# 113 matmuls of constants put between the work of a two-layer recurrent block

## The chip, the cores and the metric

The kernel runs on one core of one Trainium2 chip. The metric is the time of one execution in device microseconds (us). The engines are named as in the profile: PE is TensorE (PEld its weight loads), DVE VectorE, ACT ScalarE, POOL GpSimd, SP the queue that issues most DMAs.

## The reference

The input x has shape (2, 2048, 256) in fp32. There are two layers; each normalises x, sends it through two branches, and adds the product of the first with the silu of the second. Cut to what matters:

```python
xn = layernorm(x)
s = local_and_latent_attention(xn)          # 16 heads, window 128
g = silu(mixture_of_experts(xn))            # 8 experts, each token goes to one
x = x + s * g
xn = layernorm(x)
s = block_attention_and_mlp(xn)             # 16 heads, blocks of 64, MLP of 1024
g = silu(two_layer_local_transformer(xn))   # 8 heads of 64, window 128, depth 2
x = x + s * g
```

All arithmetic is fp32.

## The kernel before

The 4096 tokens are 32 tiles of 128 rows (NT), taken in 8 groups of four tiles (NG, GT). The program has three stages, one after another:

1. The first layer (lines 379 to 960). For every group `head` projects queries, keys and latents, `attention` scores and sums, tile by tile and half tile by half tile; `prep` normalises, transposes and routes the tokens; `route` works out each token's place; `send` scatters the normalised rows, one tile per indirect DMA on POOL (L547), into expert order; `expert` runs 39 expert tiles beside the attention of the later groups.
2. The dense branch of the second layer (968 to 1366), two transformer layers with 16 rounds of four tiles in all (NR, NM = 64 tiles): `gate_head` forms the input of a round, `prepare` projects and rotates a tile, `attention` and `forward` follow.
3. The attention branch of the second layer (1379 to 1647): again `head`, `attention`, `forward` in 8 rounds, and the store of the output.

The passage from stage 1 to 2 and from 2 to 3 is what the change's short name calls a change of branch.

The order of instructions on every engine is the order in which the program records them; no scheduler moves them. It is made by `in_turn` (L90): it takes lanes, each with a start a, an end b and a list of steps with weights, gives each step the place a + (b - a) x (weight so far + half its own) / (sum of weights), sorts all steps of all lanes by that place, and runs them. The unit is a round, so a lane (0, 1, ...) spreads over the first one. Every engine works its own list strictly in that order, and waits for others by semaphores.

```python
order.append((a + (b - a) * (at + w / 2) / total, i, len(order), do))
...
for _, _, _, do in sorted(order, key=lambda x: x[:3]):
    do()
```

PSUM is dealt out by `bank` (L43): tiles named acc have 2 buffers, all others (s for matmul results, tp for transposes) share 6 in rotation, so that the seventh tile waits until the first was read. A constant array cst (128 x 448: the identity and two masks) is the first load of the program (L48).

```python
def bank(tag):
    return ps.tile([P, 512], F32, name=tag, tag="acc" if tag == "acc" else "b", bufs=2 if tag == "acc" else 6)
```

Lines that the prediction names. Stage 1: L445 transposes of normalised rows; L453 router logits; L489 counts for the route; L204 and L214 projections of queries and keys; L682, L698, L711 and L735 latents; L228 values; L114 scores; L107 mask and row minimum on DVE (tiles pr, mn, mnl); L136 exponentials on ACT; L151 transposes of the weights; L71 and L69 copies out of PSUM on DVE and ACT (tile pt); L165 weighted sums; L188, L252 and L261 the way to the output; L580 the experts' input. Stage 2: L368 transposes of a round's input; L1087 and L1103 projections; L1066 transposes; L1120 and L1131 rotation and row norm on POOL; L341 the gather of expert rows; L1189 division; L1280 transposes, L1297 and L1319 the two halves of the MLP (tile h2T its input). Stage 3: rg is the load of a group, L1425 its transposes, L1601 and L1614 the MLP.

Of the kernel before, what the change touches and what calls it, by code (L numbers as in the profile page):

```python
# [14 lines left out]
NT = B * S // P  # L15
# [3 lines left out]
NG = NT // GT  # L19
# [11 lines left out]
def kernel(ctx: ExitStack, tc: tile.TileContext, io: dict, col: dict):  # L31
    nc = tc.nc
# [14 lines left out]
    cst = sb(const, [P, io["cst"].shape[1]], "cst")  # L47
# [15 lines left out]
    ysort = rmem.tile([FT * P, D], F32, name="ysort")  # L63
    ati = const.tile([P, NT], I32, name="ati", tag="ati")


    def copy(i, out, in_):
        if i % 2:
# [21 lines left out]
    def in_turn(*lanes):  # L90

        order = []
        for i, (a, b, lane) in enumerate(lanes):
            total, at = sum(w for w, _ in lane), 0.0
            for w, do in lane:
                order.append((a + (b - a) * (at + w / 2) / total, i, len(order), do))
                at += w
        for _, _, _, do in sorted(order, key=lambda x: x[:3]):
            do()
# [279 lines left out]
    with ExitStack() as l0_ctx, tc.manual_schedule(engines=ordered):  # L379
# [49 lines left out]
        def prep(g):  # L429

            d = {}
            xg = xn[:, g * GT : (g + 1) * GT, :]
            xT = xT_of(g)
            o = oh[:, g * GT : (g + 1) * GT, :]

            def moments(t):
                if not t:
                    d["mv"] = sb(xp, [P, GT, 2], "ln_mv", 3)
                    d["rs"] = sb(xp, [P, GT], "ln_rs", 3)
                ln_moments(xp, d["mv"], t, [xg[:, t, :]])  # L440

            def turn(c):
                tp = bank("tp")
                for t in range(GT):
                    nc.tensor.transpose(tp[:, t * P : (t + 1) * P], xg[:, t, c * P : (c + 1) * P], ident)  # L445
                copy(c, xT[:, c, :], tp)

            def logits():

                lg = d["lg"] = bank("s")[:, 0 : GT * E].rearrange("p (t e) -> p t e", t=GT)  # L450
                for t in range(GT):
                    for k in range(2):
                        nc.tensor.matmul(  # L453
                            lg[:, t, :],
                            lhsT=xT[:, k, t * P : (t + 1) * P],
                            rhs=wr[:, k, :],
                            start=(k == 0),
                            stop=(k == 1),
                        )
                mx = sb(xp, [P, GT], "mx", 2)  # L460
                nc.vector.tensor_reduce(mx, lg, AX.X, ALU.max)
                nc.vector.tensor_tensor(o, lg, bc(mx, 2, [P, GT, E]), ALU.is_equal)
                nc.vector.tensor_tensor(o, o, bc(desc, 1, [P, GT, E]), ALU.mult)
                nc.vector.tensor_reduce(mx, o, AX.X, ALU.max)
                nc.vector.tensor_tensor(o, o, bc(mx, 2, [P, GT, E]), ALU.is_equal)

            lane = [(1, lambda t=t: moments(t)) for t in range(GT)]
            lane += [(1, lambda: ln_rsqrt(d["rs"], d["mv"], 1e-5)), (2, lambda: None)]
            lane += [(1, lambda t=t: normalize(xg[:, t, :], xg[:, t, :], d["mv"], d["rs"], t)) for t in range(GT)]
            lane += [(1, lambda c=c: turn(c)) for c in range(2)] + [(1, lambda: None), (1, logits)]  # L470
            return lane
# [380 lines left out]
        def finish(n):  # L852

            d = outs[n]

            def take():
                acc = accs.pop(n)
                d["aT"] = sums_out(pa, acc)
                zs = zss[n]
                nc.vector.tensor_scalar(zs, zs, 1e-30, None, ALU.max)  # L860
                nc.vector.reciprocal(zs, zs)

            def divide():
                d["o"] = divided(pa, d["aT"], zss.pop(n))

            lo = lambda: d["o"].rearrange("p b v s d -> p (b v s) d")

            def weigh():
                d["g1"] = sb(pa, [P, 16, 16], "g1")
                nc.gpsimd.tensor_tensor(d["g1"], lo(), bc(gl, 1, [P, 16, 16]), ALU.mult)  # L870
                nc.gpsimd.tensor_tensor(d["g1"], d["g1"], d["g2"], ALU.add)
                nc.gpsimd.tensor_tensor(lo(), lo(), d["rem"], ALU.subtract)

            def gate():
                d["gate"] = sb(pa, [P, 16], "gate")
                nc.vector.tensor_reduce(d["gate"], d["g1"], AX.X, ALU.add)
                nc.scalar.activation(d["gate"], d["gate"], AF.Exp, scale=-1.0)

            def mix():
                nc.vector.tensor_scalar(d["gate"], d["gate"], 1.0, None, ALU.add)  # L880
                nc.vector.reciprocal(d["gate"], d["gate"])
                nc.vector.tensor_tensor(lo(), lo(), bc(d["gate"], 2, [P, 16, 16]), ALU.mult)
                nc.gpsimd.tensor_tensor(lo(), lo(), d["rem"], ALU.add)

            def back():
                d["oT"] = turned_out(pa, d["o"].rearrange("p b v s d -> p b (v s d)"))

            def out():
                s = sb(pa, [P, D], "s")
                nc.vector.tensor_tensor(s, times_out(d["oT"], outw), bout, ALU.add)  # L890
                nc.sync.dma_start(rows_s[:, n, :], s)
                del outs[n]

            return [take, divide, weigh, gate, mix, back, out]
# [27 lines left out]
                lane += [(0.4, back), (0.7, none), (0.3, ahead[1]), (0.7, none), (0.5, out), (0.5, none)]  # L922
            return lane

        in_turn((0, 1, prep(0)), (0.5, 1.5, prep(1)), (0.9, 1.8, head(0)))
        project_values(0)
        score(0)
        score(1)
# [6 lines left out]
        for g in range(NG):  # L935
            lanes = [(0, 1, attention(g))]
            if g < NG - 1:
                lanes.append((0.05, 0.75, head(g + 1)))
            if g == 0:
                lanes += [(0.3 * k, 0.3 * k + 0.35, prep(2 + k)) for k in range(3)]  # L940
            if g == 1:
                lanes += [(0.16 * k, 0.16 * k + 0.25, prep(5 + k)) for k in range(3)]
                lanes += [(0.6, 0.68, route()), (0.7, 1, sends[0:11])]
            if g == 2:
                lanes.append((0, 0.56, sends[11:]))
                lanes.append((0.57, 0.62, [(1, open_experts)] + [(1, lambda: expert_load(0))]))
            share, due = [], weight * shares[g]
            while flow and (due > 0 or g == NG - 1):
                due -= flow[0][0]
                share.append(flow.pop(0))  # L950
            if share:
                lanes.append((1 - shares[g] if g == 2 else 0, shares[g] if g == NG - 1 else 1, share))
            if g == NG - 2:
                lanes.append((0.5, 1, [(1, lambda: load_wqkv(0))]))
            if g == NG - 1:
                (_, fetch), *rest = gate_head(0)
                lanes += [(0.3, 0.4, [(1, fetch)]), (0.77, 1, rest)]
            in_turn(*lanes)
        for step in ends[NT - 1]:
            step()  # L960
# [7 lines left out]
    with tc.tile_pool(name="pd", bufs=2, side="left") as pd, tc.manual_schedule(engines=ordered):  # L968
# [374 lines left out]
            return lane  # L1343

        load_rest()
        in_turn((0, 1, prepare(0)), (0.8, 1.8, prepare(1)))
        score(0)
        lanes = []
        for r in range(NR):
            lanes.append((r, r + 1, attention(r)))  # L1350
            ahead = [prepare(m) for m in range(GT * r + 2, min(GT * r + GT + 2, NM))]
            if r == NG - 1:

                ahead.insert(2, [(0, lambda: load_wqkv(1)), (8, lambda: None)])
            if r == NR - 1:
                ahead.append([(1, lambda j=j: turn_tile(NM - 1, j)) for j in range(2)])
            lanes.append((r, r + (1 if r < NR - 1 else 0.5), sum(ahead, [])))
            if r < NR - 1:
                lanes.append((r, r + 0.45, gate_head(r + 1)))
            if r < NR - 3:  # L1360
                lanes.append((r + 1.25, r + 2.65, forward(r)))
        lanes += [(NR - 1.75, NR - 0.56, forward(NR - 3)), (NR - 0.75, NR - 0.24, forward(NR - 2))]
        lanes.append((NR - 0.24, NR, forward(NR - 1, 0, 2)))
        in_turn(*lanes)
        in_turn((0, 0.5, finish(NM - 1)), (0, 1, forward(NR - 1, 2, 1)))
        in_turn((0, 1, forward(NR - 1, 3, 1)))
    cw_qkv = sb(wq, [P, 2, 3 * D], "d_wqkv")
    nc.sync.dma_start(cw_qkv, io["L1_attn_w_qkv"].rearrange("(k p) n -> p k n", p=P))
    cw_out = sb(wd, [P, 2, D], "d_wo")
# [9 lines left out]
    with tc.tile_pool(name="pc", bufs=2, side="left") as pc, tc.manual_schedule(engines=ordered):  # L1379
# [249 lines left out]
            lane += [(0, lambda t=t: again(t)) for t in ts]  # L1629
            return lane + [(3.4, lambda t=t: narrow(t)) for t in ts]  # L1630

        in_turn((0, 1, head(0)))
        project_values(0)
        score(0)
        score(1)
        lanes = []
        for g in range(NG):
            lanes.append((g, g + 1, attention(g)))
            if g < NG - 1:
                lanes.append((g + 0.02, g + 0.72, head(g + 1)))  # L1640
            if g < NG - 3:
                lanes.append((g + 1.27, g + 2.6, forward(g)))
        lanes += [(NG - 1.73, NG - 0.6, forward(NG - 3)), (NG - 0.73, NG - 0.25, forward(NG - 2))]
        lanes.append((NG - 0.24, NG, forward(NG - 1, 0, 2)))
        in_turn(*lanes)
        in_turn((0, 0.6, [(1, step) for step in ends[NT - 1]]), (0, 1, forward(NG - 1, 2, 1)))
        in_turn((0, 1, forward(NG - 1, 3, 1)))


def _constants():  # L1650
# [141 lines left out]
```

## Time and profile before

| | |
|---|---|
| time, median of 3 runs | 3057.86 us (3057.32 to 3060.87) |
| time of the profiled execution | 3057.81 us |
| its span, first to last instruction | 3056.0 us |
| mean granted clock of TensorE | 0.947 |
| busy: PE, PEld | 2743.0 us (90%), 1979.2 us (65%) |
| busy: DVE, ACT, POOL | 1884.3 (62%), 1675.5 (55%), 1064.8 us (35%) |
| matmul records | 28250, of 15996 matmuls |

An fp32 matmul leaves two records, a transpose one. The page gives each engine's busy time, then the span in 40 equal slices of 76 us, each digit a tenth; the row PEclk is the clock that TensorE was granted. Where a view gives a row as `line engine op x count`, the count is of records. Waits are put down to what ended them.

### The profile page before, as it was taken

How to read it: one execution, taken by the hardware profiler on the slowest of the kernel's cores; microseconds unless marked ns; L12 is line 12 of the kernel's file. 1: busy time of each engine (PE TensorE's matmuls, PEld its weight loads, DVE VectorE, ACT ScalarE, POOL GpSimd, SP SyncE). 2: the span in 40 equal slices, each digit the busy share in tenths (PEclk: the TensorE clock that was granted, in tenths of full speed). 3: DMA queues.
4: the chain of work that ended last, by engine and by line, in shares of the span. 5: the costliest groups of instructions: out<-in, count | busy, mean ns of one | idle time of the engine just before them, and what ended most of it. 6: DMA issues, size and time to landing. Idle time of an engine off the chain costs nothing.

```text
span 3056.0 us, 72578 instructions
## 1 busy us (share of the span) xinstructions
PE 2743.0 (90%) x28250; PEld 1979.2 (65%) x28250; DVE 1884.3 (62%) x6708; ACT 1675.5 (55%) x4598; POOL 1064.8 (35%) x1227
## 2 busy tenths in 40 slices
PE   7875999999985789999999999999998689999997
PEld 4553888888872556656666666666666556666666
DVE  6774555556553777776676676666665366665542
ACT  4554666768772444444444444555553367776772
POOL 1224233323333554554443443444342112222212
PEclk8887999999996899999999999999999889999999
DMA  5002322222212010110000010000000100010000
GB/s 173 14 28 70 132 96 93 100 95 96 100 60 83 26 29 22 29 29 27 14 19 29 15 38 8 8 8 5 2 5 15 53 15 13 25 32 22 19 15 21
DMA packets 88417, 128.63 MB, mean 42 GB/s; under 512 B 8173, under 2 KB 78220, under 8 KB 83084
## 3 DMA queue, kind: packets, MB, share of 16 engines
q1 hardware_dynamic: 85004, 115.60, 11.8%
q0 software_dynamic: 3072, 8.39, 0.9%
q8 instruction: 225, 3.69, 0.5%
q14 instruction: 116, 0.95, 0.1%
HBM read 88.58 MB, written 27.00 MB: 38 GB/s over the span
## 4 chain that ended last, share of the span: by engine, by line
PE 30%; DVE 6%; issue 6%; POOL 4%; ACT 4%; DMA 0%; SPq 0%; POOLq 0%; DVEq 0%; ACTq 0%
PE s L1297 7%; PE s L1319 3%; PE s L1087 3%; ACT pr L1490 3%; PE s L1614 2%; PE s L1601 2%; PE s L1215 2%; POOL inv L1131 1%; PE s L1103 1%; PE acc L1042 1%; POOL scr L1120 1%; PE s L1012 1%; PE tp L151 1%; PE s L214 1%; PE tp L1066 1%
## 5 line engine op out<-in xcount | busy, mean ns | idle before, releaser
L1032 ACT ACTIVATE pr<-pr,mn 128x192 f32<-128x192 f32 (+2 forms) x512 | 188.6, 439 | 276.2 <-DVE mn L107 275.9
L1131 POOL TENSOR_TENSOR inv<-inv,nhalf 128x16 f32<-128x16 f32 x64 | 188.4, 2944 | 414.3 <-DVE inv L1130 414.3
L107 DVE CUSTOM_DVE_ANT_0 pr<-s,cst 128x128 f32<-128x128 f32 (+2 forms) x1024 | 261.6, 316 | 92.2 <-PE s L1470 71.4
L1297 PE MATMUL s<-h2T,d_w 128*128 128x512 f32 (+2 forms) x792 | 314.8, 552 | 0.6 <-DVE h2T L1287 0.6
L69 ACT COPY pt<-tp 128x384 f32<-128x384 f32 (+3 forms) x320 | 156.4, 495 | 247.3 <-PE tp L151 227.4
L151 PE MATMUL tp<-cst,pr 128*128 128x128 f32 x1488 | 220.0, 285 | 60.9 <-ACT pr L1032 51.2
L136 ACT ACTIVATE pr<-pr,mn 128x192 f32<-128x192 f32 (+2 forms) x512 | 222.8, 436 | 71.2 <-DVE mn L107 70.8
L1490 ACT ACTIVATE pr<-pr,mn 128x128 f32<-128x128 f32 x512 | 198.1, 388 | 111.0 <-DVE mn L107 110.7
L1120 POOL TENSOR_TENSOR scr<-scr,tab 128x512 f32<-128x512 f32 x128 | 176.9, 1382 | 201.7 <-DVE scr L71 201.6
L151 PEld LDWEIGHTS tp<-cst,pr 128*128 128x128 f32 x1488 | 180.2, 147 | 101.6 <-ACT pr L1032 56.9
L1087 PE MATMUL s<-d_wqkv,hT 128*128 128x512 f32 x512 | 245.4, 623 | 0.0
L71 DVE COPY pt<-tp 128x384 f32<-128x384 f32 (+3 forms) x320 | 181.6, 567 | 101.6 <-PE tp L151 72.9
L1297 PEld LDWEIGHTS s<-h2T,d_w 128*128 128x128 f32 x792 | 143.5, 194 | 141.5 <-issue 135.4
L1310 DVE SCALAR_TENSOR_TENSOR u<-s,cols,ge 128x512 f32<-128x512 f32 (+2 forms) x108 | 73.9, 689 | 199.4 <-PE s L1297 124.2
L1319 PE MATMUL s<-d_w,u 128*128 128x256 f32 x768 | 178.0, 382 | 0.0
L165 PE MATMUL acc<-pt,v 64*32 64x128 f32 x4992 | 125.3, 294 | 44.6 <-DVE pt L71 28.5
L1087 PEld LDWEIGHTS s<-d_wqkv,hT 128*128 128x128 f32 x512 | 98.8, 204 | 99.5 <-issue 98.7
L611 PE MATMUL s<-Wo,it 128*128 128x128 f32 x1248 | 159.5, 283 | 0.8 <-ACT it L603 0.8
L1319 PEld LDWEIGHTS s<-d_w,u 128*128 128x128 f32 x768 | 142.8, 190 | 22.3 <-issue 3.1
L611 PEld LDWEIGHTS s<-Wo,it 128*128 128x128 f32 x1248 | 150.1, 196 | 9.1 <-issue 7.1
L1619 POOL TENSOR_TENSOR y<-y,stream 128x256 f32<-128x256 f32 x32 | 23.4, 730 | 370.4 <-DVE y L1618 370.4
L107 DVE CUSTOM_DVE_ANT_0 pr<-s,cst_a 128x192 f32<-128x192 f32 (+2 forms) x512 | 144.0, 347 | 8.9 <-PE s L114 6.6
(271 smaller groups left out, 6406.9 us busy)
## 6 DMA issues: line engine op xcount, KB each, us to landing
w<-in_W1b_dram SPq DMA_DIRECT2D x39, 1028.0 KB
xsort<-zero SPq DMA_DIRECT2D x1, 4992.0 KB
xs<-xsort SPq DMA_DIRECT2D x39, 128.0 KB
ysort<-ys SPq DMA_DIRECT2D x39, 128.0 KB
xn<-in_L_attn_x_dram SPq DMA_DIRECT2D x8, 512.0 KB
rows_s<-s SPq DMA_DIRECT2D x32, 128.0 KB
stream<-in_L_attn_x_dram SPq DMA_DIRECT2D x8, 512.0 KB
sg<-rows_s SPq DMA_DIRECT2D x8, 512.0 KB
```

The lines of the kernel that those rows point to most:

```text
L71: nc.vector.tensor_copy(out, in_)
L107: nc.vector.tensor_tensor_reduce(pr, sc, mask, 1.0, CAP, ALU.add, ALU.min, mn)
L136: nc.scalar.activation(w, w, AF.Exp, bias=mn[:, v : v + 1], scale=-1.0, accum_out=zs[:, v, blk, s : s + 1])
L151: nc.tensor.transpose(tp[:, k * P : (k + 1) * P], pr[:, k, :, :].rearrange("p v j -> p (v j)"), ident)
L611: nc.tensor.matmul(mm, lhsT=d["it"][:, ic, :], rhs=late["Wo"][:, ic, h], start=(ic == 0), stop=(ic == FF // P - 1))
L1032: nc.scalar.activation(p, p, AF.Exp, bias=mn[:, w : w + 1], scale=-1.0)
L1087: nc.tensor.matmul(mm, lhsT=heads[r][:, k, t * P : (t + 1) * P], rhs=wqkv_d[l][:, k, j * INNER : (j + 1) * INNER], start=(k == 0), stop=(k ...
L1120: nc.gpsimd.tensor_tensor(d["r2"][:, :, :, 32 * hf : 32 * hf + 32], d["qk"][:, :, :, 32 - 32 * hf : 64 - 32 * hf], bc(d["tab"][:, 2:4, hf, ...
L1131: nc.gpsimd.tensor_tensor(inv.rearrange("p a h -> p (a h)"), inv.rearrange("p a h -> p (a h)"), nhalf, ALU.pow)
L1297: nc.tensor.matmul(mm, lhsT=w1[l][:, k, c, :], rhs=d["h2T"][:, k, 0:w], start=(k == 0), stop=(k == 1))
L1319: nc.tensor.matmul(mm[:, 0:D], lhsT=d["u"][:, c, i * P : (i + 1) * P], rhs=w2[l][:, c, :], start=(c == 0), stop=(c == HC - 1),)
L1490: nc.scalar.activation(w, w, AF.Exp, bias=mn[:, v : v + 1], scale=-1.0, accum_out=zs[:, v, blk, st : st + 1])
```

## The change

A function `idle` is added: one matmul of the identity with all 448 columns of cst, into a bank of the rotation, read by nothing. `idles(a, b, n)` makes a lane of n of them between the places a and b. Such lanes are added to twelve calls of `in_turn`: 8 matmuls in the first call of stage 1, 16 in each of its first two rounds, 10 in the third and 6 in the last; 8, then 12 in stage 2's start and first rounds, 4 and 4 in its last two calls; 8, then 14 in stage 3's start and first rounds, 4 and 3 in its last two calls. That is 113, and TensorE's list grows from 15996 to 16109 matmuls. Nothing is removed, and the order of all other instructions stays. Of the 113, 35 stand before the first scatter L547 in the order of the program, and 15 more before the first expert tile.

```diff
+    def idle():
+
+        nc.tensor.matmul(bank("s")[:, 0:448], lhsT=ident, rhs=cst[:, 0:448], start=True, stop=True)
+
+    def idles(a, b, n):
+        return a, b, [(1, idle)] * n
...
-        in_turn((0, 1, prep(0)), (0.5, 1.5, prep(1)), (0.9, 1.8, head(0)))
+        in_turn(idles(0, 0.4, 4), (0, 1, prep(0)), (0.5, 1.5, prep(1)), (0.9, 1.8, head(0)), idles(0.7, 1.8, 4))
...
+            if g < 2:
+                lanes.append(idles(0, 1, 16))
             if g == 2:
+                lanes.append(idles(0, 0.6, 10))
...
-                lanes += [(0.3, 0.4, [(1, fetch)]), (0.77, 1, rest)]
+                lanes += [(0.3, 0.4, [(1, fetch)]), (0.77, 1, rest), idles(0.75, 1, 6)]
...
-        in_turn((0, 1, prepare(0)), (0.8, 1.8, prepare(1)))
+        in_turn((0, 1, prepare(0)), (0.8, 1.8, prepare(1)), idles(0.3, 1.8, 8))
...
+            if not r:
+                lanes.append(idles(0, 1.25, 12))
...
-        in_turn((0, 0.5, finish(NM - 1)), (0, 1, forward(NR - 1, 2, 1)))
-        in_turn((0, 1, forward(NR - 1, 3, 1)))
+        in_turn((0, 0.5, finish(NM - 1)), (0, 1, forward(NR - 1, 2, 1)), idles(0, 0.5, 4))
+        in_turn((0, 1, forward(NR - 1, 3, 1)), idles(0, 0.5, 4))
...
-        in_turn((0, 1, head(0)))
+        in_turn((0, 1, head(0)), idles(0.2, 0.9, 8))
...
+        lanes.append(idles(0, 1.27, 14))
...
-        in_turn((0, 0.6, [(1, step) for step in ends[NT - 1]]), (0, 1, forward(NG - 1, 2, 1)))
-        in_turn((0, 1, forward(NG - 1, 3, 1)))
+        in_turn((0, 0.6, [(1, step) for step in ends[NT - 1]]), (0, 1, forward(NG - 1, 2, 1)), idles(0, 0.5, 4))
+        in_turn((0, 1, forward(NG - 1, 3, 1)), idles(0, 0.5, 3))
```

## The prediction

> **What bounds the kernel now.** I read the page first: TensorE is busy nine tenths of the time, and the row of the granted clock is below full just where its busy row dips.
>
> ```profile
> PE   7875999999985789999999999999998689999997
> PEclk8887999999996899999999999999999889999999
> ```
>
> A slice is 76 us. The dips are the first four slices (the first layer's first rounds), slices 13 and 14 (first change of branch), 31 to 33 (second change) and the last. The clock is granted over 0.947 of the span, so (1 - 0.947) x 3056 = 162 us of full clock are missing, 324 us at half clock. Then the same by stage (columns: stretch, its length, busy time of PE, PEld, DVE, ACT, POOL, clock, DMA share, GB/s):
>
> ```profile
> 38.00:205.00 167.00, 134.79 (x1490) 96.69 (x1490) 127.09 (x574) 93.94 (x379) 30.56 (x46) 0.81 0.05 15
> 205.00:311.00 106.00, 65.64 (x813) 45.58 (x814) 54.56 (x254) 50.86 (x204) 47.04 (x56) 0.77 0.24 83
> 904.00:1005.00 101.00, 44.65 (x347) 25.64 (x345) 40.43 (x98) 22.19 (x40) 44.94 (x48) 0.68 0.24 75
> 1005.00:1077.00 72.00, 58.23 (x744) 40.05 (x744) 55.07 (x143) 30.85 (x64) 40.42 (x33) 0.93 0.09 27
> 2431.00:2546.00 115.00, 90.09 (x1006) 61.35 (x1007) 74.62 (x362) 64.51 (x272) 23.58 (x42) 0.82 0.13 39
> 3020.00:3056.00 36.00, 20.38 (x112) 17.92 (x110) 5.11 (x14) 7.05 (x19) 7.27 (x12) 0.85 0.03 12
> ```
>
> No engine is full here. In 38 to 205 TensorE and VectorE hand work to each other (81% and 76% busy); each wait of one is the other's last piece. In 205 to 311 it is neither:
>
> ```profile
> POOL xsort L547 <- DMA xsort<-xn,ati: 43.5, 26, 3.7
> ```
>
> ```profile
> PE tp L580 <- DMA xs<-xsort: 19.5, 1, 19.5
> ```
>
> These are waits of POOL and of PE in that stretch (total, times, longest). POOL's 32 scatters L547 run one after another, 2.7 us each, from 205.25 to 299; the experts' weights and xs load behind them, and PE waits 19.5 us for these. That stretch has POOL's length, whatever TensorE's clock is. So the first layer's start is worth what moves the first scatter, at 205.25.
>
> Last, the clock in steps of 3.4 us:
>
> ```profile
> 112.20:115.60 3.40, 2.55 (x74) 1.62 (x66) 3.31 (x17) 1.54 (x8) 1.61 (x3) 1.00 0.02 5
> 115.60:119.00 3.40, 1.47 (x7) 1.14 (x7) 2.83 (x17) 3.40 (x19) 0.83 (x1) 0.69 0.00 0
> 119.00:122.40 3.40, 3.40 (x22) 3.07 (x24) 2.60 (x9) 1.79 (x6) 0.27 (x1) 0.50 0.00 0
> 122.40:125.80 3.40, 3.40 (x76) 2.77 (x69) 2.39 (x18) 1.85 (x9) 0.46 (x1) 0.80 0.02 5
> ```
>
> A stretch of many small matmuls with pauses (74, mostly of L165, which the groups give as 64*32 of the array) is followed by about 7 us at half clock, and a dense stretch ends that. An added full-array matmul in the thin stretch could keep the clock.
>
> **The change: 113 matmuls, priced.** The trace has none of 448 columns; the nearest is the 512-column fp32 matmul of L1297, 16 records or 8 matmuls in 6.87 us on the chain of waits:
>
> ```profile
> 1577.64 6.87 PE s L1297 x16
> ```
>
> That is 0.859 us each, so 448 columns take 0.859 x 448/512 = 0.75 us, and 1.5 at half clock (six transposes L151 take 0.85 us at 173.7, at full clock, and 1.49 at 118.3, at half). All 113 are 85 us of PE, if nothing hid them. What they displace is read from where the changed program puts each in PE's order, and from a path that I followed back by hand in the timeline, from instruction to what released it.
>
> *To the first scatter (35 matmuls).* The path holds 74.8 us of PE, 27.2 of it at half clock: 8.8 in 38 to 59 (L781, L114 twice, L165, L204), 3.4 at 82 to 86 (L261, L214), 5.7 at 118 to 124, 0.9 at 147, 3.4 at 155 to 158 (L151, L188, L204), 4.8 at 167 to 171 (L445, L151, L214). At full clock all of it would save 13.6 us.
> [...] The half clock in 38 to 205 is (1 - 0.81) x 2 x 167 = 63 us, so 32 us would be to gain. The path says 13.6, since in the rest of the 63 us VectorE or ScalarE were last. I take the path. [...] Six added matmuls fall into thin stretches (79.8, 98.8, 115.2, 136.4, 150.9, 163.6); after 38 and after 164 one alone probably doesn't keep the next stretch. I keep 9.5 of the 13.6.
> Cost: the first 4 run before 10.7, while PE waits for data anyway; those at 16.2 and 23.5 are hidden, since VectorE waits until 23.5 for cst_a. Nine stand between two PE pieces of the path (29.6, 34.2, 62.6, 87.5, 110.2, 120.5, 156.6, 173.7, 184.8): 9 x 0.75 = 6.7. Eight stand shortly before such a piece, with a wait of 0.05 to 0.85 us ahead of it to run in: together 3.0. Twelve stand beside VectorE's or ScalarE's part of the path, with PE waits of 1 to 2.5 us behind them: nothing, and 0.75 each if that part gets shorter. Each also takes one of the six PSUM banks in turn, so what follows waits for a bank released one tile later; now such waits are 3.9 us in 38 to 205 (PE on mnl and pt), so 0 to +3.9; I take 1, as most tiles are read well before. Sum: -9.5 + 6.7 + 3.0 + 1 = +1.2 (from -5 to +10).
>
> *205 to 311 (15).* Under POOL's scatters: 0.
>
> *First change of branch (6 + 8, and 3 of the 12 in the next lanes).* The 4 at 904 to 909 precede a 9 us wait of PE on ACT, which itself waits for the gather: 0. The two before L368 and L261 (930, 932) are on the path at half clock: +1.7, and the window they fill ends the throttle one step early, -1.7. The rest up to 1005 lie beside POOL's L1120, L1131, L341 and the loads: 0 (-1 to +2).
>
> *First rounds of the dense branch.* From 1015 to 1050 PE is over nine tenths busy at full clock; nothing to win. Six matmuls are 4.5 us, the waits of PE there (on L1189 and L71) some 2 of it: +2.5 (0 to 4.5). The last three fall beside POOL's chain before 1077: 0.
>
> *Second change of branch (8 + 8 + 14).* In 2404 to 2431 four run in waits of 1.9 and 2.8 us, four between L1280 and L1297 on the path: 2.3; of 2.8 us at half clock perhaps half is lifted, -0.7: +1.6. In 2431 to 2446 PE waits 15 us for rg and the moments; five of the next eight run at the start of that wait, too early to keep the clock until 2446, and three stand in L214 and L204 on the path: +2.3. Then 14 in the first round: the path has 15 us of PE at half clock, of which three thin stretches get a matmul: -4.3; four of them are on the path and some partly: +4.0. Sum +1.6 + 2.3 - 0.3 = +3.6 (-3 to +9).
>
> *The end (7).* Four before and in L1601 at 3024: 2.0 against 1.7 for 3.4 us of half clock that they lift: +0.3. Of the last three one runs in the wait for h; two are between h2T and L1601, probably at half clock: +1.7. Sum +2 (-1 to +4).
>
> Total: 1.2 + 0 + 0 + 2.5 + 3.6 + 2 = +9.3 us. The profiled execution took 3057.81 us (its span 3056.0 and 1.8 around), the median is 3057.86: so 3067.
>
> **Rivals.**
> *The clock is held wherever a matmul was put.* Then the first layer's start gives 13.6 - 8.2 = -5.4, the first change -1, the second 0 before 2431 and 8.5 - 6 = -2.5 behind it, the end -1: -10, that is 3048. It decides from the point where a thin stretch with one more matmul counts as busy; for it: dense stretches ended the throttle each time. Against it: several thin stretches follow one another, and the pauses of 10 to 20 us stay. 22%.
> *The matmuls vanish in waits and the clock that they win is not on the path* (others last): 3058. For it: PE waits 28 us in 38 to 205. Against: nine lie between two busy pieces of PE. 20%.
> *The change doesn't do what it says, the clock stays as it is.* Then costs alone: 9.7 + 1 + 2.5 + 2.3 + 6.6 + 3.7 = 26, so 3084. 13%.
>
> **How the numbers follow.** The likeliest, 45%, is 3067, itself 3058 to 3078. A measurement of this kernel tells 0.2%, 6 us, from no change. Faster by more: the first rival and a bit of the second, 23%. Within: the rest of the second and the low end of the likeliest, 23%. Slower: 54%. The range 3049 to 3081 leaves out about a tenth on either side.
>
> **What would show it.** The mean clock should rise from 0.947 to 0.955 to 0.965, most in 38 to 205 (0.81 to about 0.9), and stay low in 904 to 1005 and 2431 to 2446. The first scatter should start at 204 to 208, and PE's wait for xs stay near 19 us. The time from 1005 to 1077 should grow by 2 to 3 us, from 2446 to 2546 by about 2. Wrong: a first scatter before 201 (the clock was worth more than the path says), or new waits of PE on PSUM readers of 5 us or more (banks).

## The result and the profile after

The changed kernel takes 3069.62 us (median of 7 runs, 3066.77 to 3076.3); before takes 3057.86 (7 runs, 3057.32 to 3061.72). The ratio is 1.0037 (95% interval 1.0025 to 1.0048), so +11.3 us (7.6 to 14.7). The forecast was +9.3. The profiled execution took 3066.77 us (span 3065.0), the lowest of the seven; what follows explains its +9.0 us of span, not the 3 us between it and the median.

The rows of TensorE and of the granted clock, in 40 slices:

```profile
PE   8886999999985899999999999999998799999997
PEclk8998999999997999999999999999999899999999
```

Slices 2 to 4, 13, 14 and 33 are a tenth higher than before: all lie where matmuls were added. The mean clock rose from 0.947 to 0.961. By stage (the columns as before: stretch, length, PE, PEld, DVE, ACT, POOL, clock, DMA share, GB/s; the ends follow the same instructions as those of before to within half a us or so, but 1077.3 and 2554.2 lie 1.2 and 1.7 us late and 3028.2 lies 1.4 us early, so lengths are to be compared in the table further down):

```profile
38.00:204.50 166.50, 139.39 (x1554) 94.37 (x1548) 128.12 (x592) 95.04 (x385) 30.57 (x46) 0.94 0.04 14
204.50:310.00 105.50, 71.53 (x843) 47.15 (x844) 54.74 (x254) 50.95 (x204) 46.93 (x56) 0.82 0.24 85
901.10:1003.00 101.90, 55.06 (x381) 29.80 (x379) 41.22 (x104) 22.82 (x42) 45.60 (x49) 0.77 0.25 77
1003.00:1077.30 74.30, 64.34 (x763) 43.16 (x764) 55.69 (x147) 31.21 (x66) 41.30 (x35) 0.94 0.09 27
2433.50:2554.20 120.70, 101.50 (x1055) 65.16 (x1054) 75.45 (x364) 66.27 (x277) 23.57 (x42) 0.90 0.12 38
3028.20:3065.00 36.80, 23.36 (x132) 18.55 (x130) 5.22 (x14) 7.05 (x19) 7.28 (x12) 0.93 0.04 15
```

The first stretch went from 0.81 to 0.94, and yet it is only 0.5 us shorter: what the clock gave, the added matmuls took (PE is 4.6 us busier at a far higher clock). The part of the program that was shown in steps of 3.4 us, its first three steps:

```profile
112.20:115.60 3.40, 3.30 (x86) 2.27 (x84) 3.31 (x13) 1.92 (x7) 2.13 (x3) 1.00 0.02 5
115.60:119.00 3.40, 2.31 (x14) 1.02 (x10) 2.98 (x21) 3.40 (x19) 0.68 (x1) 1.00 0.00 0
119.00:122.40 3.40, 3.40 (x44) 2.59 (x43) 3.19 (x10) 2.26 (x9) 0.62 (x2) 1.00 0.00 0
```

Before, the clock fell to 0.69 and 0.50 in the second and third of these. In the changed kernel a line of the program stands 7 to 12 lines further down: the scatter L547 is L554 (L558 in the kernels below that count their calls), L580 is L587, and L69 on PE is the added matmul. That matmul (duration of a record in ns, minimum, median and maximum; first and last start), and the two waits on which the forecast for 205 to 311 stood (engine, what it waited for, total, times, longest):

```profile
L69 PE MATMUL s<-cst x226: 539/539/1115, 3.4 to 3050.1; 128*128 128x448 f32 x113
```

```profile
POOL xsort L554 <- DMA xsort<-xn,ati: 45.1, 27, 2.9
```

```profile
PE tp L587 <- DMA xs<-xsort: 18.7, 1, 18.7
```

A record lasts 0.539 us, but two overlap: from the start of an added matmul to the start of the next instruction PE takes 0.754 us (median at full clock) and 1.494 at half clock. The waits are as before (43.5 and 19.5).

To see where the time came from, every instruction of VectorE, ScalarE and GpSimd was paired with the same one of before, in order; the difference of their ends, us:

| stretch of before | forecast | measured |
|---|---|---|
| to the first scatter, 205 | +1.2 | -0.5 |
| 205 to 311 | 0 | -1.0 |
| 311 to 904 (nothing added) | none | -1.5 |
| 904 to 1005 | 0 | +0.2 |
| 1005 to 1077 | +2.5 | +1.8 |
| 1077 to 2404 (nothing added) | none | +1.3 |
| 2404 to 2431 | +1.6 | +2.3 |
| 2431 to 2546 | +2.0 | +3.9 |
| 2546 to 3020 (nothing added) | none | +3.0 |
| to the end | +2 | -0.6 |
| sum | +9.3 | +9.0 |

The sum agrees; yet 4.3 us arose behind 1077 where nothing was added, and -1.5 before it, 2.8 of the 9.0 us in all. The experiments had to tell whether the terms are right or cancel by chance.

### The profile page after: what moved, and what is told of

The parts are those of the page before. It is cut to its first block, busy times and chain, and to the rows that moved or that the text cites. A ratio compares the mean times of both kernels' runs of the same rounds, so it can differ in the third digit from the quotient of the medians.

```text
span 3065.0 us, 73003 instructions
## 1 busy us (share of the span) xinstructions
PE 2799.0 (91%) x28476; PEld 1994.5 (65%) x28476; DVE 1885.1 (62%) x6708; ACT 1675.6 (55%) x4598; POOL 1065.2 (35%) x1227
## 4 chain that ended last, share of the span: by engine, by line
PE 31%; DVE 6%; issue 5%; POOL 4%; ACT 4%; DMA 0%; SPq 0%; POOLq 0%; DVEq 0%; ACTq 0%
PE s L1307 7%; PE s L1329 3%; ACT pr L1502 3%; PE s L1097 3%; PE s L1626 2%; PE s L1613 2%; PE s L1225 2%; POOL inv L1141 1%; PE s L1113 1%; PE acc L1052 1%; POOL scr L1130 1%; PE s L1022 1%; PE tp L158 1%; PE s L221 1%; PE tp L1076 1%
```

## The experiments

Where nothing else is said an experiment starts from the changed kernel. Own theory: each added matmul costs its time on PE where PE is on the path, and gives back half clock there.

**Small matmuls at the same places.** Edit:

```diff
-        nc.tensor.matmul(bank("s")[:, 0:448], lhsT=ident, rhs=cst[:, 0:448], start=True, stop=True)
+        nc.tensor.matmul(bank("s")[0:32, 0:8], lhsT=ident[0:32, 0:32], rhs=cst[0:32, 0:8], start=True, stop=True)
```

> The 113 added matmuls stay at their places and take their PSUM banks in turn, but are 32x32 of the array and 8 columns wide, so they fill no window and take little of PE. Own theory (PE's time on the path, less half clock that is lifted): no clock is won (mean clock 0.946 to 0.948) and only banks and some 0.1 us each for about 35 on the path are paid: 3059 to 3064 us. Rival (the bank rotation is the main price): about as the changed kernel, 3066 to 3072, with new waits of PE on readers of PSUM.

Measured: 3073.43 us against 3056.06 of before on this chip, ratio 1.0054 (1.004 to 1.0068), +17 us; clock 0.945. Both theories missed, the own one by far. One of these matmuls holds PE for 0.154 us; one of the same 32 by 32 with 448 columns holds it 0.11 us longer than a full one (next experiment). By stretches, against the second profile of before (below), 5.7 of its 16 us arise in 205 to 311, 2.9 in 2446 to 2546, 3.4 in 2546 to 3000, where nothing was added, and 1.5 before the first scatter, where banks were to be short. So something acted that neither theory held; the experiments on banks and on fetches, below, find the same losses without these matmuls.

**The same time on a corner of the array.** Edit: `[0:32, 0:448]`, `ident[0:32, 0:32]` and `cst[0:32, 0:448]` in that call.

> The 113 added matmuls keep their 448 columns and so their time on PE (0.75 us), but use 32x32 of the 128x128 array. Own theory (the clock goes by how much of the array works in a window, and the 17 us that it gives back are on the path): clock 0.945 to 0.95, time 3058 + 26 = 3084 us (3078 to 3090). Rival A (the clock that is won is not on the path): as the changed kernel, 3067 to 3072, at the clock of before. Rival B (PE's busy time counts, whatever part of the array works): as the changed kernel, 3067 to 3072, at a clock of 0.96.

Measured: 3110.94 us, ratio 1.0171 (1.0157 to 1.0185), +55 us, clock 0.944. These are the corner's 226 records and its stretch up to the first scatter, at 216.3:

```profile
L69 PE MATMUL s<-cst x226: 534/558/952, 3.1 to 3092.1; 32*32 32x448 f32 x113
```

```profile
38.00:216.30 178.30, 159.60 (x1572) 97.29 (x1568) 129.37 (x593) 95.33 (x385) 30.56 (x47) 0.83 0.04 13
```

PE is busier than in the changed kernel (159.6 against 139.4 us) and the clock is 0.83, not 0.94: how much of the array works decides here, not how long PE is busy. Rivals A and B fall. (The clock falls also behind stretches in which PE works: in the kernel before, in the 3.41 us up to the fall, 113.49 to 116.90, PE is busy for 2.16, mostly with L165, which uses 64 by 32 of the array. In the corner kernel half clock even follows two windows, from 177.8 and 198.2, in which PE is busy throughout.) The size was wrong: 26 expected, 55 measured. One corner matmul holds PE for 0.864 us at full clock, 0.11 more than a full one (0.754); what takes the 0.11 is not shown. If all 113 paid it in full that would be 12 us. The rest: costs alone are larger than the sum had them. Against the second profile of before (below) the corner kernel lost 11.6 us up to the first scatter, about as priced, but also 6.2 in 205 to 311, where nothing was expected and the scatters take 97 us in place of 91, 5.3 in 904 to 1005, 14.0 in 2404 to 2546 and 9.9 at the end, where it has 27.5 us of half clock and the changed kernel 5.5.

**Both kernels once more.**

> The changed kernel once more, for a second profile of it. In the first one half-clock stretches at 2653, 3008 (here and not before) and 431 (before and not here) moved the stage times by 1.5 to 1.7 us each, where nothing was added. Theory (the place of the clock's windows against the program is chance): such stretches in the long stages differ again, while 1003 to 1077 and 2404 to 2460 keep their +2 and +5 us. Rival (the change moves them): the same stretches at the same places. Time 3067 to 3073 either way.

> The kernel before once more, for a second profile of it. Theory (the windows' place is chance): its stretches of half clock in 311 to 904 and 2546 to 3020 differ by one or two from those of the first profile, 1.6 us each. Rival: the same at 430.9, none between 2546 and 3000. Time 3057 to 3062 either way.

Measured: 3067.42 us, ratio 1.0035 (1.0026 to 1.0044), and 3057.3 (one execution). The half-clock stretches of the changed kernel were at the same places again (2653.9 and 3008.9), so the theory of chance does not hold for them. Before was not the same twice: the 3.4 us at 430.9 were gone, and between 2404 and 2431 it had 10.2 us of half clock in place of 3.4. Against its first profile the second gained 1.6 us in 205 to 250 and 2.0 in 425 to 700, and lost 3.3 in 2404 to 2431, with no change at all. So the 311 to 904 row of the table (-1.5) is the first profile's chance, and 2404 to 2431 is +2.3 against the one and -1.0 against the other.

**Banks alone.** Edit: the body of `idle` is `bank("s")`, with no matmul.

> At each of the 113 places only a PSUM bank of the rotation is taken, with no matmul. Own theory (banks cost 1 to 4 us, nearly all before the first scatter): 3057 to 3062. Rival (the shifted rotation is what the 32x32 matmuls of 8 columns paid, 17 us): 3065 to 3074.

Measured: 3060.08 us against 3061.34 (this chip), ratio 0.9998 (0.999 to 1.0007): nothing. As a price of the change the rival falls, and the +1 for banks in the sum is within the noise. But the profile of this kernel is one of its slowest execution (3066.44 us), and in it 2.9 us arise in 2446 to 2546 and 3.4 in 2546 to 3000, the amounts that the small matmuls had there, with half clock at 2651.5. No matmul is added here, so losses at these places don't prove a cost of one.

**The first 35 alone, and 26 of them.** Edit: `idle` counts its calls and acts for k < 35; in the second kernel not for the nine that were counted on the path.

```diff
+        k = count[0]
+        count[0] += 1
+        if k < 35 and k not in [6, 7, 12, 16, 20, 22, 28, 30, 32]:
```

> Only the 35 added matmuls that stand before the first scatter are kept, 78 are left out. Own theory (gain and cost cancel on the path to the first scatter): first scatter at 204 to 206 us, clock of 38 to 205 about 0.93, time within 2 us of before. Rival (the chance place of the clock's windows decides, each thin stretch +-1.6 us): first scatter as above, but 2 to 5 us of difference arise in the long stages behind it, where nothing is added.

> Of the 35 before the first scatter the nine that were counted as standing between two PE pieces of the path are left out too; 26 stay. Own theory (the nine cost 6.7 us and lift little): first scatter 3 to 6 us earlier than with 35, at 199 to 202, time 3 to 6 us below the kernel with 35, so 3050 to 3055. Rival (the nine hold the clock as much as they cost): first scatter at 204 to 207, clock of 38 to 205 down to 0.85 to 0.9, time as with 35.

Measured: 3070.84 us for 35, ratio 1.0031 (1.0018 to 1.0045), where the own theory had no more than 2 us; 3058.23 for 26, ratio 0.9991 (0.9981 to 1.0001), where it had 3050 to 3055. The scatters' rows (duration min, median, max, then first and last start), with 35 and with 26:

```profile
L558 POOL DMA_INDIRECT xsort<-xn,ati x32: 958/970/1223, 204.6 to 301.6; - x32
```

```profile
L558 POOL DMA_INDIRECT xsort<-xn,ati x32: 958/968/1222, 202.2 to 293.5; - x32
```

The nine cost 2.4 us at the first scatter, not 6.7. Without them the clock of this stretch falls a little, from 0.93 to

```profile
38.00:202.00 164.00, 136.79 (x1530) 93.02 (x1530) 127.19 (x582) 94.40 (x383) 30.58 (x46) 0.92 0.04 14
```

The half clock in it grows from 23.0 to 25.6 us (28.6 in the second run of this kernel, below), worth 1.3 to 2.8 us if all of it were on the path. The rest of the 4.3 us between the price and the measurement stays open; some of the nine must have run in waits.

The surprise is another 5.6 us: with 35 the scatters take 97 us from first to last, with 26 91. POOL's wait for them is 50.6 us instead of 43.7. Three neighbouring scatters with 35 (start, length, then the idle time before and what ended it), and the DMA queues between the second and the third:

```profile
226.77 0.98 POOL L558 DMA_INDIRECT xsort<-xn,ati  x1 [0.94 <-DMA xsort<-xn,ati]
230.88 0.96 POOL L558 DMA_INDIRECT xsort<-xn,ati  x1 [3.12 <-DMA xsort<-xn,ati]
233.55 0.96 POOL L558 DMA_INDIRECT xsort<-xn,ati  x1 [1.71 <-DMA xsort<-xn,ati]
```

```profile
q0 software_dynamic: 48, 0.13, 9.3%
q8 instruction: 1, 0.02, 1.9%
```

The first lasted 4.1 us until the next could start, where 2.7 is usual, and in it lies one 16 KB packet of the instruction queue q8: 225 to 227 such packets in a run, where TensorE has 57,700 to 58,100 weight loads, matmul and semaphore records, so one for every 256 of its instructions (called a block below). In the first profiles of before and of the changed kernel (57,657 records, 225 packets; 58,082 and 227) packet number k, counted from 0, begins when TensorE has started 256 k + 148 to 331 of these records, from the first packet to the last: so the packets are put down to TensorE, and called its fetches. Over the 14 profiles of this study there are 350 gaps between scatters that nothing else lengthens (25 of 31 in each). When the fetch began, us after the scatter's issue, against the median gap:

| fetch begins | none | 0 to 0.5 | 0.5 to 1 | 1 to 1.3 | 1.3 to 1.7 | 1.7 to 2.1 | 2.1 to 2.5 | later |
|---|---|---|---|---|---|---|---|---|
| gaps | 282 | 9 | 7 | 5 | 19 | 4 | 16 | 8 |
| median us | 2.69 | 2.87 | 3.21 | 3.90 | 4.17 | 2.73 | 2.70 | 2.75 |

Where nothing is hit the scatter's own packets run from 1.5 to 2.05 us after its issue. Of 31 gaps over 3.5 us 30 hold a fetch. With 35 six scatters are hit, with 26 none is: there the fetches come, for instance, 2.29 us after the issue. The 113 small matmuls have five hits and 96.5 us of scatters. This is a correlation, so it was tried directly.

**Fetches moved by half a block.** Edit, on the kernel with 35 and on the kernel before: 32 of the small matmuls (128 instructions) at the very start of stage 1, where PE waits for data.

```diff
+        for _ in range(32):
+            nc.tensor.matmul(bank("s")[0:32, 0:8], lhsT=ident[0:32, 0:32], rhs=cst[0:32, 0:8], start=True, stop=True)
```

> The kernel with only the 35 added matmuls before the first scatter, and 32 more of 32x32 and 8 columns at the very start of TensorE's list, where it waits for data until about 10 us: they move every 16 KB fetch of TensorE's instructions by half a block (128 instructions, some 5 us) and cost next to nothing. Theory (fetches that fall on a scatter's packets hold it up by 1.2 to 2 us; with the 35 this happened six times): first to last scatter 91 to 94 us in place of 97, time 2 to 6 us below that with the 35 alone, 3061 to 3066 where that one had 3067 to 3071. Rival (the 35 hold the scatters up in another way): first to last scatter 96 to 98, time as with the 35.

> The kernel before with the same 32 small matmuls at the very start of TensorE's list. Theory (fetches): first to last scatter changes from 91 to 93 us, likely to 93 to 97, time up by 0 to 5 us. Rival (fetches don't matter): 91 to 93 as in the two profiles of before, time within 1.5 us of before.

Measured: 3064.99 us, ratio to before 1.0017 (1.001 to 1.0024), where 35 alone had 1.0031; and 3065.81, ratio 1.0024 (1.0014 to 1.0033), that is +7.3 us, more than the 0 to 5 expected. The scatters of the two, and for comparison those of before:

```profile
L558 POOL DMA_INDIRECT xsort<-xn,ati x32: 958/968/1223, 206.4 to 300.8; - x32
```

```profile
L547 POOL DMA_INDIRECT xsort<-xn,ati x32: 958/969/1222, 207.5 to 304.6; - x32
```

```profile
L547 POOL DMA_INDIRECT xsort<-xn,ati x32: 958/969/1256, 205.3 to 297.9; - x32
```

94.4 us with 35 (97 before the shift; 91 to 94 expected), 97.1 for the kernel before (92.7 and 91.1 without the shift), and the waits of POOL in the latter are

```profile
POOL xsort L547 <- DMA xsort<-xn,ati: 51.3, 27, 3.5
```

On the kernel before, where nothing else is added, this shows it for the scatters: five of their gaps are 4.2 to 4.8 us, each with a fetch 1.4 to 2.2 us in. The 32 were not free, though: the first scatter comes 1.8 us later with 35 and 2.3 to 2.8 later on the kernel before, so not all of the +7.3 us is the fetches'. On the kernel with 35 the scatters take less time, but in the whole the step is not shown: the two ratios, each against its own runs of before, have intervals that overlap.

**Second change of branch alone; first change and first dense round alone.** Edits: `idle` acts for 76 <= k < 106, and for 50 <= k < 76.

> Only the 30 added matmuls of the second change of branch are kept (8, 8 and the 14 of the first round behind it). Own theory (they cost where they stand): +5 to +6 us between 2404 and 2546, as in the changed kernel, and +0 to +2 behind it: time 3061 to 3065. Rival (the 3 us at 2653 and 3008 came with the shift of the program against the clock's windows by whatever was added before): +5 to +6 between 2404 and 2546, and the half-clock stretches behind it at other places or none.

> Only the 26 added matmuls of the first change of branch and of the dense branch's first round are kept. Own theory: 0 up to 1005, +2 to +3 from 1005 to 1080, 0 behind it: time +1 to +4 us. Rival (what comes between 1077 and 1300 in the changed kernel, 1 us, and later, belongs to these too): +3 to +6.

Measured: the 30 are +5.2 us, ratio 1.0017 (1.001 to 1.0023); in their profile 2404 to 2546 is +3.3 us against the second profile of before (+6.6 against the first), and no stretch of half clock at 2653, as its rival had forecast. The 26 are +3.7 us, ratio 1.0012 (1.0004 to 1.002); their profile has +1.9 in 1005 to 1077, as the changed kernel's two have (+1.8 and +1.7, all against the first profile of before), and it was already 2.4 us behind that profile at 904, when hardly any of them had run.

Alone, the 35, the 30 and the 26 come to 9.5 + 5.2 + 3.7 = 18 us by their ratios, against 11.3 for all 113: the parts don't add up, and 5.3 of the 7 us between are the scatters, which the 35 alone delay more than the whole change does.

**26 of the first 35 again.**

> The 26 added matmuls that do not stand between two TensorE pieces of the path to the first scatter, once more, for a narrower interval. Own theory: 3 us below before (first scatter 2.5 us earlier, the same 91 us of scatters), ratio 0.998 to 1.0. Rival (the 3 us were chance of the fetches and of the clock's windows): ratio 0.999 to 1.002, with first to last scatter at 93 to 97.

Measured: 3056.07 us against 3058.47, ratio 0.9994 (0.9986 to 1.0002), first scatter at 201.8, the last 91.6 us later. The own theory's stretch is there; over the two runs the gain is some 2 us, and neither interval excludes none.

## Why the forecast was right, step by step

The forecast was right in sign and size (+9.3; +11.3 by the ratio), and so was the price of one matmul (0.75 and 1.5 us forecast, 0.754 and 1.494 measured). The sum is better than its terms: their errors cancel in part.

- *To the first scatter* (+1.2 forecast; -0.5 and +0.1 in the two profiles of the changed kernel against the first of before): right. Its two sides come near too: in the corner kernel, where the clock is not won, the first scatter comes 11.1 us late (costs were put at 10.7), in the changed kernel 11.5 earlier than that (gain kept: 9.5). Up to 3.9 us of both may be the time that a corner matmul holds PE longer, 0.11 us for each of 35, so the sides are less sure than the sum. By half of the half-clock time the gain would be 20 us: the corner kernel has 59.0 us of half clock in this stretch, the changed one 19.3. The path was the better price. That one matmul alone would not keep the clock after 38 and after 164, on which the 9.5 rests, was an estimate; the changed kernel has half clock from 42.2 to 49.0 (38.4 to 58.9 before) and none from 164.7 to 171.5, where all was half clock before. Within the costs the nine were mis-sized: 2.4 us net, not 6.7. That they should only cost was a slip, but the clock that they hold explains only a part of it.
- *205 to 311: "That stretch has POOL's length, whatever TensorE's clock is."* The number, 0, holds here (91.7 us of scatters; 92.7 and 91.1 before). The reason is incomplete: TensorE's instructions act on POOL's scatters through their fetches, and with the first 35 alone, at the same first scatter, the scatters take 5.3 us longer than in the changed kernel. That the change came out near 0 was luck of where its fetches fall.
- *904 to 1005* (0; +0.2) and *1005 to 1077* (+2.5; +1.8): right; +1.9 when those 26 are alone. The half clock that begins at 912 ends at 929.6 in place of 936.1.
- *Second change* (+3.6; +6.2 against the first profile of before, +2.8 against the second): that they cost is right, the 30 alone take 3.1 to 7.0 us by the ratio. Where they do is less sure: the path was read from one profile of before that happened to be the quicker one in 2404 to 2431, and in 2446 to 2546 the banks alone showed 2.9 us in one profile.
- *The end* (+2; -0.6 in both profiles): wrong. The step "two are between h2T and L1601, probably at half clock: +1.7" failed: all seven run at full clock, 0.754 us each, and the half clock around them shrinks from 10.5 to 5.5 us (the clock is 0.93 instead of 0.85). In the corner kernel the end costs +10; the matmuls here earn their time.
- *What was in no step*: +1.3 in 1077 to 2404 and +3.0 in 2546 to 3020, with half clock at 2653 and twice the length at 3008. The prediction put nothing on stretches without an added matmul. At 2653 it is the place of the clock's windows that decides (below); what moved it, the matmuls or their banks, stays open.

Of the signs named: the mean clock 0.961 (0.955 to 0.965), the first scatter at 204.8 (204 to 208), PE's wait for xs 18.7 (near 19) and the clock of 904 to 1005 that stays low (0.77, from 0.68) came true. 38 to 205 went beyond what was named (0.94, not about 0.9), 1005 to 1077 grew a little less (1.8; 2 to 3), 2446 to 2546 more (4.0; about 2). No new wait on PSUM readers shows. The first rival (3048) falls on the time, although the clock was held in most places. The second (3058) falls with the corner, whose lost clock is on the path. The third, "costs alone", lost as the clock did change; its size of 26 was far too small, and so were the gains.

## What to carry to other kernels

A filler matmul earns its place only where it runs inside a wait that is not the last one and lifts half clock from path work behind it: price both on the path, and try leaving out those between two busy pieces (without nine of the 35 the first scatter came 2.4 us earlier). When instructions are added to one engine, look also at which transfers its instruction fetches fall on, above all a chain of small transfers that is itself the path (here 5.6 us of scatters, between 35 added matmuls and 26). And take two profiles of the kernel before: differences of 3 us in a stretch can be its own (3.3 us here in 2404 to 2431).

## What the runs showed of the hardware

**Fetches.** A 16 KB instruction fetch of about 1 us (median 0.96 us before, 1.01 in the changed kernel) that begins 0.5 to 1.7 us after a scatter's issue goes with a gap 0.5 to 1.5 us longer in the median (3.21 to 4.17 us against 2.69). Whether TensorE waits for the fetches was not measured. The scatters are held up here: with 35, where six are hit, they take 5.6 us longer than with 26. Why a fetch does this is not shown: no view tells which DMA engine carried it.

**The clock's windows.** In each trace all beginnings of clock stretches lie on one grid of 3.413 us. Where the grid lies at the program's start differs from run to run (0.26 to 3.13 us in 14 profiles). But against the work at 2404 us it no longer differs. Counted in grid steps from the first edge after the start (lines of the kernel before):

| profile | first edge, us | POOL L883 at 200 | POOL L1316 at 2404 | POOL L1580 at 3038 |
|---|---|---|---|---|
| before | 0.85 | 58.51 | 705.21 | 889.83 |
| before again | 0.36 | 58.51 | 704.21 | 889.81 |
| before, fetches moved | 3.13 | 58.51 | 706.25 | 891.82 |
| changed | 1.21 | 58.28 | 705.21 | 892.55 |
| changed again | 1.78 | 58.28 | 705.20 | 892.58 |
| first 35 | 0.73 | 58.36 | 707.21 | 891.84 |
| 26 of them | 2.54 | 57.12 | 704.21 | 889.82 |
| second 30 | 2.77 | 58.55 | 704.24 | 890.81 |

In all 14 profiles L1316 stands 0.20 to 0.25 of a step behind an edge. Counted on this grid, a delay or a gain on the way there arrives as whole steps of 3.4 us, or not at all. A likely reason, worked out from this grid and from the 0.754 and 1.494 us of a matmul, and not tried by itself: work that begins δ later within half clock ends only δ/2 later if the clock rises at a fixed edge, so each such stretch halves the offset. It would explain why runs of one kernel spread over 9 us (before: 3052.8 to 3061.9 in 15 runs on one chip) and why the 1 to 3 us of single steps could not be found in the medians.

How little decides a window shows at 2653. There PE waits 1.9 us for ACT. In nine profiles the window of 3.4 us with that wait holds 1.71 to 1.81 us of PE work, and the clock stays full. In four, the changed kernel's two, the small matmuls and the banks alone, the grid lies some 0.2 to 0.7 us otherwise against the program, the window holds 1.52 or 1.53 us, and half clock follows for 3.4 us, worth half of it, 1.7. (In the corner kernel it lies elsewhere.) In all four all 113 banks were taken, and in none of the nine; whether that sets the place of the grid was not tried by itself.
